# Zero-padding three small stationary operands to 128x128, and storing dt*x in three pieces, in a two-layer Mamba and outlook kernel

## The chip, the cores and the metric

The kernel runs on one core of a Trainium2 chip. The metric is the device time of one execution in microseconds (us); lower is better. Engines are named as the profile names them: PE (TensorE matmuls), PEld (its weight loads), DVE (VectorE), ACT (ScalarE), POOL (GpSimd) and SP, whose queue issues all DMAs of this kernel.

## The reference

The input x is (4, 384, 64, 64) in fp32. Two layers follow one another, each added to its input. The first is a selective state space layer (Mamba) over the 4096 pixels of an image taken as a sequence; the second is outlook attention, which the change does not touch. The first, cut to what matters:

```python
xz = einsum('blc,dc->bld', xn, in_proj_w)          # xn: normalised x; 2 x 768 channels
xb, z = split(xz, 2)
xc = silu(causal_conv4(xb) + conv_b)               # 768 channels
x_dbl = einsum('bld,ed->ble', xc, x_proj_w)        # 24 (dt) + 16 (B) + 16 (C)
dt = softplus(einsum('blr,dr->bld', x_dbl[..., :24], dt_w) + dt_b)
Bm, Cm = x_dbl[..., 24:40], x_dbl[..., 40:]
# for each time step, per channel d and state n (16 of them):
#   h = exp(dt * A) * h + (dt * xc) * Bm ;  y = sum_n h * Cm
y = (y + xc * D) * silu(z)
out = einsum('bld,cd->blc', y, out_proj_w)
```

## The kernel before, in words

**Tiling.** Each of the 4 images is cut into 17 chunks of 241 pixels (TM), 68 chunks in all. The 768 inner channels are NJ = 6 blocks of 128. A chunk is scanned in NU = 12 units of 64 channels; for one unit the scan state h is a tile of 128 partitions (4 states x 32 channels) by 8 segments of 242. The main loop runs over stages s, one unit per stage: DVE multiplies half of dt*x with B (`s_inputs2`), DVE scans (`s_scan`), POOL multiplies the other half with B (`s_inputs`) and the result with C (`s_outputs`), ACT makes the decay exp(dt*A) (`s_decay`), and at every odd stage PE sums h over the states for two units into a PSUM tile y (`s_sum`). The tiles h rotate through five buffers, so a multiply that begins a new h waits for the y matmuls that read the old one.

**Front work.** Everything that a chunk needs before its scan is put among the stages of earlier chunks by a dictionary written out by hand, `plan`. A key (r, part) gives a stage r, counted from two chunks before the chunk's own scan, and a place in it: EARLY, READY, SCAN, POOL, MID, LATE, in this order. As the chunk is 12 stages long, stages 18 and 6, for instance, fall together for two chunks. The entries that matter:

```python
(13, POOL): [at(f_silu, "xc", "zs")],
(14, POOL): [f_bc],
(15, EARLY): [f_xd],
(16, READY): [at(f_dt, 0)],
(16, SCAN): [at(f_dt, 1)],
(17, EARLY): [at(f_dt, 2)],
(17, READY): [at(f_plog, 0)],
(17, MID): [at(f_dtx, 0)],
(18, EARLY): [at(f_plog, 1)],
(18, SCAN): [at(f_dtx, 1), at(f_plog, 2)],
(19, READY): [at(f_dtx, 2)],
```

Every engine runs its instructions in the order of the program (`keep_in_program_order`).

**The steps.** `f_bc` multiplies xc with the x_proj weights wx into 56 rows of the PSUM tile px (ps_xd in the profile), six matmuls. `f_xd` has ACT copy these rows to the SBUF tile xd; rows 0 to 31 of it are B and C, 32 to 55 are dt, and the rest of its 64 rows stay at the 1.0 of a memset, so that row 56 carries the bias. `f_dt` (dt0, dt1, dt2 below) multiplies rows 32 to 56 of xd with wdt, two blocks at a time, into ps_dt; ACT takes the exponential. `f_plog` and `f_log` complete the softplus. `f_dtx` multiplies dt by xc on DVE, two blocks at a time, and after the third call the whole tile is stored to DRAM (dxd) with four DMAs of 32 partitions each, by `f_store`; `f_log` stores dt (dtd) in the same way. `f_b` spreads rows of B over 128 partitions by a matmul of xd with a 0/1 operand sel into bp. In the same stages lie `f_var` of a later chunk (ps_var, matmuls with one moving column), and `e_project` of an earlier one (ps_out). In fp32 the profile shows two matmul records for each matmul of the program.

**DMA order.** `s_fetch` brings dtx and dt of four 32-channel groups from DRAM to the layout of the scan (dxr, dtr), eight DMAs at every even stage, four units ahead of their scan, three buffers deep. All DMAs go through SP in program order. PSUM tiles of the front work (tag "mm") rotate through two buffers.

Of the kernel before, what the change touches and what calls it, by code (L numbers as in the profile page):

```python
# [7 lines left out]
F32 = mybir.dt.float32  # L8
# [4 lines left out]
P = 128  # L13
C = 384
NCB = C // P
DI = 768
NJ = DI // P
NS = 16
RK = 24
KC = 4  # L20
TM = 241
CG = 32
NQ = DI // CG
NG = NS // 4
# [55 lines left out]
def mamba_layer(ctx, tc, x, w, x1, sc1, bi1, consts, behind):  # L80
# [17 lines left out]
    pe, ve, ae, gp, sp = (  # L98
        InOrder(tc, e) for e in (nc.tensor, nc.vector, nc.scalar, nc.gpsimd, nc.sync)
    )  # L100
# [5 lines left out]
    wf = fronts.enter_context(tc.tile_pool(name="wf", bufs=1, side="right"))  # L106
    iof = fronts.enter_context(tc.tile_pool(name="iof", bufs=3, side="right"))
    front = fronts.enter_context(tc.tile_pool(name="front", bufs=1, side="right"))
# [3 lines left out]
    dram = ctx.enter_context(tc.tile_pool(name="dscr", bufs=3, space=bass.MemoryType.DRAM))  # L112
# [5 lines left out]
    def load(name, shape, pool=wp):  # L118
        t = pool.tile(shape, F32, tag=name, name=name)
        sp.dma_start(t, w[name])  # L120
        return t
# [62 lines left out]
    sp.dma_start(win[:, :, :DI], w["win"][:, :, :DI])  # L184
    cw = load("cw", [P, NJ, KC], wf)
    cbias = load("cbias", [P, NJ], wf)
    wx = load("wx", [P, NJ, 2 * NS + RK], wf)


    KX = 2 * NS + RK + 1  # L190
    xd = wf.tile([2 * CG, 1 + TM], F32, tag="xd", name="xd")
    gp.memset(xd, 1.0)
    wdt = wf.tile([KX, DI], F32, tag="wdt", name="wdt")
    sp.dma_start(wdt[2 * NS :, :], w["wdt"])
    alog = load("alog", [P, NQ, NG])
    sel = load("sel", [2 * NS, NG // 2, P], wf)

    cdiag = wf.tile([P, NJ, KC, P], F32, tag="cdiag", name="cdiag")
    ddiag = wp.tile([P, NJ, P], F32, tag="ddiag", name="ddiag")
# [190 lines left out]
    def f_bc(c):  # L390

        t = c.t
        px = pmm.tile([P, 2, TM], F32, tag="mm", name="ps_xd")
        for j in range(NJ):
            pe.matmul(
                px[: 2 * NS + RK, 0, :t], wx[:, j, :], c.xc[:, j, 1:], start=(j == 0), stop=(j == NJ - 1)
            )
        c.px = px

# [10 lines left out]
    def f_dt(c, jj):  # L410
        t = c.t
        if jj == 0:
            c.dt = front.tile([P, NJ, TM], F32, tag="dt", name="dt")
        pp = pmm.tile([P, 2, TM], F32, tag="mm", name="ps_dt")
        for h in range(2):
            j = 2 * jj + h
            pe.matmul(
                pp[:, h, :t], wdt[2 * NS :, j * P : (j + 1) * P], xd[2 * NS : KX, 1:], start=True, stop=True
            )
        ae.activation(c.dt[:, 2 * jj : 2 * jj + 2, :t], pp[:, :, :t], AF.Exp)  # L420

    def f_store(v, name):

        d = dram.tile([NJ, CG, 4, TM], F32, tag=name, name=name)
        for q in range(4):
            sp.dma_start(d[:, :, q, :].rearrange("j c t -> c j t"), v[CG * q : CG * (q + 1)])
        return d

    def f_log(c):

        t = c.t
        ae.activation(c.dt[:, :, :t], c.dt[:, :, :t], AF.Ln, bias=one)
        c.dtd = f_store(c.dt, "dtd")
# [15 lines left out]
    def f_b(c):  # L449

        for g in range(ND):
            pe.matmul(bp[:, g, : c.t], sel[:, g, :], xd[: 2 * NS, 1:], start=True, stop=True)

    def f_plog(c, jj):

# [2 lines left out]

    def f_dtx(c, jj):
        if jj == 0:  # L460
            c.dtx = front.tile([P, NJ, TM], F32, tag="dtx", name="dtx")
        ve.tensor_mul(c.dtx[:, 2 * jj : 2 * jj + 2, :], c.pl, c.xc[:, 2 * jj : 2 * jj + 2, 1:])
        if jj == NJ // 2 - 1:
            c.dxd = f_store(c.dtx, "dxd")

# [3 lines left out]
    def at(f, *args):  # L471
# [26 lines left out]
# [10 lines that stand above are left out]
        (19, POOL): [f_log],  # L508
        (19, MID): [f_spread],
# [52 lines left out]
    bp = pbb.tile([P, 2, TM], F32, tag="bp", name="bp")  # L562
# [188 lines left out]
    w_bias(NJ, 2 * NJ)  # L751
    w_scale(1)
    f_bc(first)
    f_xd(first)
    f_spread(first)
    for jj in range(NJ // 2):
        f_dt(first, jj)
    f_b(first)
    f_var(third)
    f_root(third)  # L760
# [15 lines left out]
    for s in range(-4, NU * (len(chunks) + 2)):  # L776
        k, m = divmod(s, NU)
# [53 lines left out]
class OutlookTile:  # L831
# [11 lines left out]
    def load(self, sp, x1, xr):  # L843

        c, W = self, self.W
        for cb in range(NCB):
            sp.dma_start(
                xr[:, cb, c.lo :, :],
                x1[c.b, :, (2 * NR * c.t + c.lo - 1) * W : (2 * NR * c.t + ROWS - 1) * W].rearrange(
                    "(p cb) (r w) -> p cb r w", cb=NCB, w=W  # L850
                )[:, cb],
            )
        self.xr = xr
# [357 lines left out]
def layers(ctx, tc, w, out):  # L1211
# [26 lines left out]

    started = []
    mamba_layer(tc, x.rearrange("b c h w -> b c (h w)"), w, x1, sc1, bi1, consts, behind)  # L1240
    outlook_layer(tc, x1, w, out, sc1, bi1, weights, ready)


def layouts(inputs):

    import numpy as np

    g = {k: np.asarray(v) for k, v in inputs.items()}
    c = np.ascontiguousarray

    def inner(v):
        v = v.reshape(NJ, P, *v.shape[1:])
        return c(np.swapaxes(v, 0, 1))

    a = {}
    a["x"] = c(g["x"])
    a["lnw"] = c(g["L0_conv_ln_w"].reshape(P, NCB))
    a["lnb"] = c(g["L0_conv_ln_b"].reshape(P, NCB))
    a["win"] = c(g["L0_conv_in_proj_w"].T.reshape(P, NCB, 2 * DI))
    a["cw"] = inner(g["L0_conv_conv_w"].reshape(DI, KC))  # L1260
    a["cbias"] = inner(g["L0_conv_conv_b"])
    wx = g["L0_conv_x_proj_w"]
    a["wx"] = inner(np.concatenate([wx[RK:], wx[:RK]], 0).T)
    a["wdt"] = c(np.concatenate([g["L0_conv_dt_w"].T, g["L0_conv_dt_b"][None]], 0))
    a["alog"] = c(
        g["L0_conv_A_log"].reshape(NQ, CG, NG, 4).transpose(3, 1, 0, 2).reshape(P, NQ, NG)
    )
    a["dvec"] = inner(g["L0_conv_D"])
    a["wout"] = c(inner(g["L0_conv_out_proj_w"].T).reshape(P, NJ, P, NCB).transpose(0, 1, 3, 2))

    wa = g["L1_conv_attn_w"].reshape(HEADS * KK, KK, C).swapaxes(0, 1).reshape(-1, C)
    a["wa"] = c(wa.T.reshape(P, NCB, -1))
    ab = g["L1_conv_attn_b"].reshape(HEADS * KK, KK).T.reshape(1, -1)
    a["ab"] = c(np.repeat(ab, P, 0))
    a["wv"] = c(g["L1_conv_conv_w"].reshape(KK, C, C).transpose(2, 0, 1).reshape(P, NCB, KK, C))
    wpr = g["L1_conv_proj_w"].T.reshape(NCB, P, P, NCB)
    a["wpr"] = c(wpr.transpose(1, 0, 3, 2))
    a["pb"] = c(g["L1_conv_proj_b"].reshape(P, NCB))
    f = np.float32
    a["ident"] = np.eye(P, dtype=f)  # L1280
    a["avg"] = np.full((P, P), 1.0 / C, f)
    a["blk12"] = np.kron(np.eye(P // 4, dtype=f), np.full((4, 4), 1.0 / 12.0, f)).astype(f)
    a["onesc"] = np.full((P, 1), 1.0 / C, f)
    r = np.arange(P)
    k = np.arange(2 * NS)
    a["sel"] = c(
        np.stack([(k[:, None] == 4 * i + r[None, :] // CG).astype(f) for i in range(NG // 2)], 1)
    )
    a["own"] = np.repeat(np.eye(GW, dtype=f), KK, 0)
    a["ssum"] = (r[:, None] % CG == np.arange(CG)[None, :]).astype(f)  # L1290
    return a
# [16 lines left out]
```

## Time and profile before

| | us |
|---|---|
| median of 3 runs | 6283.66 |
| the runs | 6276.35, 6283.66, 6298.06 |
| span of the profiled execution | 6278.2 |
| own time of the profiled execution | not listed beside its span |
| DVE h, the scan, busy | 3452.5 |
| POOL h, product with C, busy | 3225.4 |
| POOL h, product with B, busy | 1623.6 |
| PE ps_xd / ps_dt / bp, busy | 307.9 / 253.0 / 73.3 |
| first / last ps_xd | 84.1 / 4917 |

The profile is of one execution. "Busy" is the time in which an engine works on such instructions; idle time before a group is put down to whatever came last. The granted clock of PE is given per stretch, with 1.00 as full speed. In the timeline, each line has a start, a duration, the engine, the operation, the tiles as out<-in, the number of instructions merged, and in brackets the idle time ahead of it with its releaser. Sizes of matmul operands are written 25*128 for 25 rows by 128 columns of weights. Stretches and timelines below are in us from the start of the span.

### The profile page before, as it was taken

To read this page: it belongs to the slowest core of one execution; us is meant where nothing else is said; L and a number is where in the kernel's file an instruction comes from. 1 tells how busy PE (TensorE), PEld (TensorE's weight loads), DVE (VectorE), ACT (ScalarE), POOL (GpSimd) and SP (SyncE) were. 2 spreads that over 40 slices of the span, in tenths; PEclk is the share of its full clock that TensorE was granted. 3 is DMA by queue.
4 is the path that set the end of the run, shared out by engine and by line. 5 is a ranking of instruction groups with operands and counts; after the bars stand their busy time and mean duration, and the time that the engine had idled before them with its cause. 6 is when DMAs were issued, how large, how long until landed. Compare 5 with 4: busy or idle time off the path is not lost. (4 is left out here: it accounts for less than half of the span.)

```text
span 6278.2 us, 113454 instructions
## 1 busy us (share of the span) xinstructions
PE 5607.8 (89%) x40506; PEld 3965.2 (63%) x40506; DVE 5371.6 (86%) x4786; ACT 4990.9 (79%) x11842; POOL 5308.6 (85%) x2047
## 2 busy tenths in 40 slices
PE   6888988888888889988888888899888789999999
PEld 5666666666666666666666666666666455555555
DVE  4999999999999999999999999999999954445444
ACT  3888898888888888989888889888898845444544
POOL 3999999999999999999999999999999944433333
PEclk9999999899999999999999999999999899999999
DMA  4555555545555645555555545455545644454554
GB/s 128 133 134 147 146 135 133 133 129 143 147 138 132 146 129 138 146 132 136 141 137 147 140 126 136 129 134 139 135 125 135 167 149 162 165 170 165 173 169 146
DMA packets 640843, 894.22 MB, mean 142 GB/s; under 512 B 130249, under 2 KB 535163, under 8 KB 640148
## 3 DMA queue, kind: packets, MB, share of 16 engines
q1 hardware_dynamic: 640276, 886.96, 51.8%
q8 instruction: 319, 5.23, 0.4%
q14 instruction: 248, 2.03, 0.1%
HBM read 660.89 MB, written 225.70 MB: 141 GB/s over the span
## 5 line engine op out<-in xcount | busy, mean ns | idle before, releaser
L45 DVE TENSOR_TENSOR_SCAN h<-da,h 128x968 f32<-128x968 f32 x1632 | 3452.5, 2158 | 83.4 <-issue 48.5
L45 ACT ACTIVATE da<-dtr,aneg 128x241 f32<-128x241 f32 x6528 | 3036.8, 465 | 296.1 <-DVE h L45 133.5
L45 POOL TENSOR_TENSOR h<-h,bc 128x1928 f32<-128x1928 f32 x816 | 3225.4, 3953 | 12.7 <-DVE h L45 8.0
L45 POOL TENSOR_TENSOR h<-dxr,bc 128x964 f32<-128x964 f32 x816 | 1623.6, 1990 | 116.4 <-PE y L45 95.3
L45 PE MATMUL ps_in<-u,win 128*128 128x241 f32 x4896 | 1078.8, 374 | 83.4 <-DVE dtx L45 75.9
L45 PEld LDWEIGHTS ps_in<-u,win 128*128 128x128 f32 x4896 | 911.9, 191 | 248.2 <-DVE dtx L45 100.1
L45 POOL TENSOR_TENSOR bd<-ain,own 99x1188 f32<-99x1188 f32 x192 | 413.4, 2181 | 726.5 <-DMA ain<-ad 550.6
L45 DVE TENSOR_TENSOR h<-dxr,bp 128x964 f32<-128x964 f32 x816 | 931.6, 1142 | 109.2 <-PE y L45 93.8
L45 PE MATMUL y<-h,ssum 128*32 128x241 f32 x13056 | 907.2, 406 | 28.6 <-POOL h L45 27.7
L45 PEld LDWEIGHTS y<-h,ssum 128*32 128x32 f32 x13056 | 434.7, 119 | 442.8 <-issue 213.2
L45 PE MATMUL ps_cv<-xb,cdiag 128*128 128x241 f32 x3264 | 694.2, 368 | 5.7 <-ACT neg L45 4.7
L45 PEld LDWEIGHTS ps_cv<-xb,cdiag 128*128 128x128 f32 x3264 | 611.4, 189 | 78.5 <-issue 13.5
L45 PE MATMUL psv<-wv,xp 128*128 128x384 f32 x1728 | 592.8, 495 | 7.2 <-issue 7.2
L45 PE MATMUL ps_xd<-xc,wx 128*56 128x241 f32 x816 | 307.9, 559 | 323.1 <-ACT xc L45 323.1
L45 ACT ACTIVATE bd<-ain,own 99x324 f32<-99x324 f32 x704 | 334.6, 556 | 264.6 <-PE ps L45 240.6
L45 PE MATMUL ps_out<-zs,wout 128*128 128x241 f32 (+1 forms) x2448 | 537.2, 369 | 0.0
L45 DVE TENSOR_TENSOR fold<-fold,ps 128x192 f32<-128x192 f32 (+1 forms) x768 | 211.3, 303 | 333.2 <-PE ps L45 318.8
L45 PEld LDWEIGHTS ps_out<-zs,wout 128*128 128x128 f32 x2448 | 470.5, 192 | 36.5
L45 PEld LDWEIGHTS psv<-wv,xp 128*128 128x128 f32 x1728 | 322.7, 191 | 232.3 <-issue 18.1
L45 PEld LDWEIGHTS ps_xd<-xc,wx 128*56 128x56 f32 x816 | 154.6, 199 | 464.1 <-ACT xc L45 348.5
L45 ACT COPY vst<-psv 128x384 f32<-128x384 f32 x279 | 130.8, 470 | 322.3 <-PE psv L45 322.3
L45 PE MATMUL ps_dt<-xd,wdt 25*128 25x241 f32 x816 | 253.0, 436 | 113.5 <-ACT dt L45 80.4
(108 smaller groups left out, 5503.2 us busy)
## 6 DMA issues: line engine op xcount, KB each, us to landing
dxr<-dxd SPq DMA_DIRECT2D x1632, 120.5 KB
dtr<-dtd SPq DMA_DIRECT2D x1632, 120.5 KB
bc<-bcd SPq DMA_DIRECT2D x544, 120.5 KB
vin<-vd SPq DMA_DIRECT2D x384, 148.5 KB
vd<-vst SPq DMA_DIRECT2D x93, 576.0 KB
dxd<-dtx SPq DMA_DIRECT2D x272, 180.8 KB
dtd<-dt SPq DMA_DIRECT2D x272, 180.8 KB
xs<-in_x SPq DMA_DIRECT2D x96, 256.0 KB
```

Of the source, the lines that this page charges most:

```text
L45: return self.tc.keep_in_program_order(issue(*args, **kwargs))
```

## The change

The weights of x_proj (wx) get 72 zero columns, so that ps_xd has 128 rows; the weights of dt (wdt) get 32 zero rows ahead and 71 behind, and B's spread (sel) gets 96 zero rows behind, so that both multiply all 128 rows of xd, which grows to 128 partitions. ACT still copies 56 rows of ps_xd. The tile dtx becomes three tiles of two blocks in two buffers; each is stored with four DMAs as soon as it is written, where one store of the whole had followed the third.

```diff
-    wx = load("wx", [P, NJ, 2 * NS + RK], wf)
-    KX = 2 * NS + RK + 1
-    xd = wf.tile([2 * CG, 1 + TM], F32, tag="xd", name="xd")
+    wx = load("wx", [P, NJ, P], wf)
+    xd = wf.tile([P, 1 + TM], F32, tag="xd", name="xd")
     gp.memset(xd, 1.0)
-    wdt = wf.tile([KX, DI], F32, tag="wdt", name="wdt")
-    sp.dma_start(wdt[2 * NS :, :], w["wdt"])
+    wdt = load("wdt", [P, DI], wf)
     alog = load("alog", [P, NQ, NG])
-    sel = load("sel", [2 * NS, NG // 2, P], wf)
+    sel = load("sel", [P, NG // 2, P], wf)
...
-                px[: 2 * NS + RK, 0, :t], wx[:, j, :], c.xc[:, j, 1:], start=(j == 0), stop=(j == NJ - 1)
+                px[:, 0, :t], wx[:, j, :], c.xc[:, j, 1:], start=(j == 0), stop=(j == NJ - 1)
...
-                pp[:, h, :t], wdt[2 * NS :, j * P : (j + 1) * P], xd[2 * NS : KX, 1:], start=True, stop=True
+                pp[:, h, :t], wdt[:, j * P : (j + 1) * P], xd[:, 1:], start=True, stop=True
...
-    def f_store(v, name):
-
-        d = dram.tile([NJ, CG, 4, TM], F32, tag=name, name=name)
+    def store(v, d):
         for q in range(4):
             sp.dma_start(d[:, :, q, :].rearrange("j c t -> c j t"), v[CG * q : CG * (q + 1)])
+
+    def f_store(v, name):
+
+        d = dram.tile([NJ, CG, 4, TM], F32, tag=name, name=name)
+        store(v, d)
         return d
...
-            pe.matmul(bp[:, g, : c.t], sel[:, g, :], xd[: 2 * NS, 1:], start=True, stop=True)
+            pe.matmul(bp[:, g, : c.t], sel[:, g, :], xd[:, 1:], start=True, stop=True)
...
     def f_dtx(c, jj):
         if jj == 0:
-            c.dtx = front.tile([P, NJ, TM], F32, tag="dtx", name="dtx")
-        ve.tensor_mul(c.dtx[:, 2 * jj : 2 * jj + 2, :], c.pl, c.xc[:, 2 * jj : 2 * jj + 2, 1:])
-        if jj == NJ // 2 - 1:
-            c.dxd = f_store(c.dtx, "dxd")
+            c.dxd = dram.tile([NJ, CG, 4, TM], F32, tag="dxd", name="dxd")
+        dtx = front.tile([P, 2, TM], F32, tag="dtx", name="dtx", bufs=2)
+        ve.tensor_mul(dtx, c.pl, c.xc[:, 2 * jj : 2 * jj + 2, 1:])
+        store(dtx, c.dxd[2 * jj : 2 * jj + 2])
```

## The prediction

> **What bounds the kernel now.** I read the page first, then the busy time by stretch, the waits, and the timelines of two chunks.
>
> ```profile
> span 6278.2 us, 113454 instructions
> PE 5607.8 (89%) x40506; PEld 3965.2 (63%) x40506; DVE 5371.6 (86%) x4786; ACT 4990.9 (79%) x11842; POOL 5308.6 (85%) x2047
> ```
> ```profile
> 219.00:4841.00 4622.00, 4092.64 (x26733) 3029.72 (x26733) 4466.78 (x3362) 4121.19 (x9997) 4533.31 (x1617) 0.93 0.53 137
> ```
>
> The second fence is one stretch, the first layer in steady state; its columns are the length, then busy us of PE, PEld, DVE, ACT and POOL, the granted clock and DMA. POOL is busy 4533/4622 = 98%, DVE 97%, PE 89%. So the shares alone say that faster matmuls are worth nothing, and that at most the last 2% of POOL can be won. Who causes it is in the waits (total us, times, longest):
>
> ```profile
> POOL h L45 <- PE y L45: 95.3, 88, 8.1
> DVE h L45 <- PE y L45: 93.8, 111, 6.2
> ```
>
> The scan state h comes free only when the matmuls into y have read it, so a late y holds both full engines at once. By place in the chunk, 53.3 us of DVE's 93.8 are 39 waits at one spot, the y of stage 17, behind the last ps_dt; 30.2 us are waits of mostly 0.42 us two stages on, behind dtx and ps_in; the rest is the start. The distance from one chunk's ps_xd to the next is 71.4 us in chunks without the first wait and 71.4 plus that wait in the others (mean 72.2). So 53 us is what the changed matmuls can win there.
>
> Why is y late? A chunk with a wait of 1.24 us, PE first, then DVE and POOL:
>
> ```profile
> 937.64 4.48 PE L45 MATMUL ps_xd<-xc,wx 128*56 128x241 f32 x12 [4.75 <-ACT xc L45]
> ...
> 950.29 1.08 PE L45 MATMUL ps_dt<-xd,wdt 25*128 25x241 f32 x4 [1.19 <-ACT dt L45]
> 951.29 2.32 PE L45 MATMUL ps_var<-onesc,sq 128*121 128x1 f32 x12
> 953.55 1.97 PE L45 MATMUL ps_dt<-xd,wdt 25*128 25x241 f32 x4
> 955.44 1.17 PE L45 MATMUL y<-xc,ddiag 128*128 128x241 f32 x2
> 956.55 2.75 PE L45 MATMUL y<-h,ssum 128*32 128x241 f32 x32
> ```
> ```profile
> 959.34 1.16 DVE L45 TENSOR_TENSOR h<-dxr,bp 128x964 f32<-128x964 f32 x1 [1.24 <-PE y L45]
> 959.47 1.98 POOL L45 TENSOR_TENSOR h<-dxr,bc 128x964 f32<-128x964 f32 x1 [0.95 <-PE y L45]
> ```
>
> The same ps_dt group takes 1.08 us and then 1.97 us. The stretches (same columns) say why:
>
> ```profile
> 361.12:364.52 3.40, 3.02 (x8) 1.72 (x9) 3.40 (x5) 3.38 (x7) 3.40 (x1) 0.50 0.00 0
> 374.78:378.18 3.40, 3.03 (x20) 2.28 (x19) 3.40 (x3) 3.24 (x9) 3.40 (x2) 1.00 0.96 260
> 378.18:381.60 3.42, 3.42 (x29) 1.59 (x32) 3.42 (x2) 3.26 (x8) 3.42 (x2) 0.50 1.03 243
> 948.21:951.62 3.41, 2.22 (x12) 1.48 (x11) 3.41 (x2) 3.31 (x9) 3.41 (x2) 1.00 0.37 83
> 951.62:955.03 3.41, 3.41 (x15) 3.06 (x14) 3.41 (x3) 3.14 (x8) 3.41 (x3) 0.50 1.03 255
> ```
>
> The granted clock halves at 378.18 and at 951.62, in nearly every chunk just here. A first halving, while PE waits for the Silu, falls on ps_xd.
>
> [...] all changes of clock lie on one grid of 3.4133 us. [...] 361.12 (3.02 us of ps_xd, 128 rows, 56 columns) is followed by full clock, 374.78 (3.03 us of ps_dt, 25 rows, and ps_var, one moving column) by half. I count each 241-column matmul as 0.208 us (32 ps_cv in 6.67 us) times its share of rows in steps of 32, ps_var as nothing. Over 1437 windows a limit of 0.38 of the window then puts 15 on the wrong side, against 54 with all rows counted full. Columns must not be weighted: ps_xd brings the clock back. Zero weights seem to count: ps_cv, whose weights are diagonal, held 1.00 over two windows (2517.1 to 2523.9). [...]
>
> **The change part by part.**
> *ps_dt, 25 to 128 rows.* Four matmuls take 1.08 us now; at the full-array spacing (ps_in, 12 in 2.6 us, 0.22 each) about 0.1 us less. dt0 waits for ACT's copy, dt1 and dt2 mostly for ACT's exponential, so only dt2's 0.1 us reaches y: 7 us in 66 chunks. The real effect is activity. A window like 948.21, with four ps_out and four ps_dt, has (4 + 4/4) x 0.208 / 3.41 = 0.30 now and 8 x 0.208 / 3.41 = 0.49 then: it stays full, ps_var keeps 1.43 us instead of 2.3 to 2.4, dt2 about 1.0 instead of 1.97. The drop comes a window later and hits only y. That case exists today: the chunk at 361.50 has y alone at half clock, ends it 20.4 us after ps_xd's start, and DVE does not wait. What remains are phases whose window holds little but four ps_dt and ps_var (4 x 0.208 / 3.41 = 0.24), which start about 11.4 to 12.4 us after ps_xd: 1 of 3.41 us, 30%, half of it where dt2 lies outside the slow window; at 1.3 us (half-clock dt2 and most of y) 0.2 to 0.4 us per chunk. I take 0.32, also because 71.36 + 0.32 = 71.68 us is 21 windows, where the phase can lock. Saved: 53 - 66 x 0.32 = **32 us**, the 7 us included.
> *ps_xd, 56 to 128 columns.* Rows are unchanged, so activity is. Weight loads grow from 126 to about 190 ns, behind matmuls. [...] ACT copies ps_xd out only at 944.8, 2.7 us after its end. Cost nothing[...].
> *bp, 32 to 128 rows.* Four matmuls per chunk, 1.08 us to about 1.0, in a full stretch: nothing.
> *dtx in three pieces.* The same 60 KB x 12 in place of 180 KB x 4, so 8 DMA issues more per chunk. Four issues take 2.24 us on SP:
>
> ```profile
> 954.69 3.08 SPq L45 DMA_DIRECT2D dxr<-dxd  x4
> 957.88 2.09 SPq L45 DMA_DIRECT2D dtr<-dtd  x4
> 967.17 2.24 SPq L45 DMA_DIRECT2D dxd<-dtx  x4
> 975.90 2.21 SPq L45 DMA_DIRECT2D dtd<-dt  x4
> ```
>
> So +4.5 us, in SP's gaps (959.97 to 967.17 and 969.41 to 975.90). The first store moves ahead of the stage-18 fetch (954.69), which now waits behind DVE's first piece (957.44 to 958.09): stores to 960.3, fetch 960.3 to 965, about 5.5 us later. Its rows are needed by POOL two stages on, about 12 us after. Pieces two and three go out at 965.5 to 970, so dxd is complete 0.6 us later than now, but the next fetch waits for dtd, issued at 975.90, anyway. Nothing in steady state. New wait: two buffers for three pieces, so the third multiply waits for the first store. It starts 8.95 us (median, 7.7 least) after the first; 0.65 + 2.24 us of that go to multiply and issue, leaving 6.0 (4.8) us to land. A store of 361 KB (x1) lands in about 2.6 us. Hidden.
> *The start, once.* Loads grow by 0.22 + 0.32 + 0.10 = 0.64 MB ahead of x; at the 300 GB/s of 35 to 40 us that is 2.1 us, and PE waits for that x (1.03 us at 40.50). Twelve store issues end at 102.0 instead of 98.9 us, and the first dxr is waited for: 3 us. Together +5 us, between 0 and +8.
>
> Sum: -32 + 5 = **-27 us**. The profiled span is 6278.2 us; no execution time of its own is shown, and the runs have 6276.35 to 6298.06 with median 6283.66, so what lies around the span is small and I carry the difference over: **6257 us**. A measurement of this kernel tells about 0.3%, 19 us, from no change.
>
> **Rivals.**
> *Padding does not wake the clock* (rows that multiply zeros do not count, or rows 57 to 127, a constant one, do not). For it: no run here has padded rows; against it: ps_cv. Then only 0.1 us per chunk is won: -7 + 5, about 6282.
> *The wait moves into dtx, slower.* The third multiply is in DVE's order just ahead of the scans, and PE's ps_in, ps_rs and y wait for it, then POOL. Decided at a store landing time of 6.0 us; at 7 us, 1.0 us x 67 = +67, so -27 + 67 = +40: 6324. For it: the moved fetch puts 0.96 MB into the queues just behind that store, and DMA is at 1.03 of its share in this stretch. Against it: the store goes first, after the stage-16 fetch is through.
> *All of the late y goes:* -53 + 5 = 6236, if ps_var or loads also count.
>
> **How the numbers follow.** Main case 0.60 (6240 to 6268), no effect on the clock 0.22 (6274 to 6291), the wait in dtx or another new wait 0.15 (6300 to 6390), all gone 0.03. Four fifths of the main case pass 6264.8. Faster 0.50, same 0.33, slower 0.17. The range 6236 to 6294 leaves the slower cases out.
>
> **What would show it.** Right: in the changed profile the clock after ps_dt is full in more windows, "DVE h <- PE y" falls by about 30 us, ps_var stays near 1.43 us for 12, POOL's share of the steady stretch rises by half a per cent. Wrong: ps_dt at 1.97 us as often as now; DVE dtx waiting for a DMA; chunk distances that stay at 72.2 us, or a new floor above 71.4.

## The result, and the profile after

The changed kernel takes 6252.41 us (median of 6 runs, 6251.12 to 6258.35) against 6280.88 us of the kernel before in the same comparison (6 runs, 6267.06 to 6298.06): **ratio 0.9957 with an interval of 0.9943 to 0.9971**, 28.5 us less. The predicted difference was 27 us, and 0.43% lies above the 0.3% that a measurement can tell. The span of the profiled execution fell by 21.6 us; that execution is the slowest of the six (6258.35 us).

The page of the changed kernel gives the span, then the busy time of each engine:

```profile
span 6256.6 us, 114424 instructions
PE 5454.4 (87%) x40506; PEld 4053.0 (65%) x40506; DVE 5368.2 (86%) x4786; ACT 4987.6 (80%) x11842; POOL 5311.0 (85%) x2047
```

PE does as many matmuls as before in 153 us less busy time; DVE and POOL do the same work in the same time. The steady stretch of the first layer (length, then busy us of PE, PEld, DVE, ACT and POOL, granted clock, DMA):

```profile
219.00:4841.00 4622.00, 3961.99 (x26848) 3125.95 (x26849) 4487.05 (x3381) 4140.50 (x10050) 4559.65 (x1625) 0.95 0.52 137
```

The clock rose from 0.93 to 0.95 and POOL from 98.1% to 98.7% of the stretch. So the 153 us of PE were worth only what they freed on the two full engines, DVE and POOL; 1.3% of POOL is still open. The waits (total us, times, longest) show what was freed and what came new:

```profile
PE ps_out L45 <- DVE dtx L45: 93.7, 50, 2.9
...
POOL h L45 <- PE y L45: 75.4, 68, 8.1
...
DVE h L45 <- PE y L45: 59.2, 88, 6.2
...
DVE dtx L45 <- ACT ps_lg L45: 19.2, 22, 2.1
...
DVE dtx L45 <- DMA dxd<-dtx: 2.8, 1, 2.8
```

Two of these in the kernel before:

```profile
DVE dtx L45 <- ACT ps_lg L45: 6.0, 4, 2.1
PE ps_out L45 <- DVE dtx L45: 5.9, 4, 4.0
```

DVE's wait for y fell from 93.8 to 59.2 us. Of the 39 waits behind the last ps_dt (53.3 us), 15 are left (13.6 us). But DVE's wait for ps_lg, 6.0 us before, is 19.2 us now: 19 of these 22 waits lie in the steady chunks, 14.9 us against 1.9 (one wait) before.

**Where the new wait comes from.** Here is PE in a chunk whose clock stays full behind ps_dt (start, us, operation, in brackets the idle time ahead and its releaser):

```profile
2100.43 1.33 PE L45 MATMUL ps_var<-onesc,sq 128*121 128x1 f32 x12
2102.31 1.08 PE L45 MATMUL ps_dt<-xd,wdt 128*128 128x241 f32 x4 [0.55 <-ACT dt L45]
...
2103.73 1.84 PE L45 MATMUL y<-h,ssum 128*32 128x241 f32 x32
2107.47 1.07 PE L45 MATMUL ps_out<-xr,ident 128*128 128x241 f32 x2 [1.90 <-DVE dtx L45]
2108.34 3.94 PE L45 MATMUL ps_out<-zs,wout 128*128 128x241 f32 x12
```

The last ps_dt takes 1.08 us where the chunk shown of before had 1.97, ps_var takes 1.33 where it had 2.32, and y is done at 2105.6, 18.6 us after the start of ps_xd (2086.96). DVE does not wait for it. Now PE is too early: the next ps_out needs one of the two "mm" buffers, which DVE frees when its first dtx multiply has read it, so PE idles for 1.90 us (this wait has 93.7 us in all; before, it had 5.9). In this trace, as in that of before, every change of the granted clock lies within 0.002 us of a grid of 3.413 us; a window is one step of it. That idle time falls into one window, the second of these three (columns as above):

```profile
2100.79:2104.20 3.41, 2.86 (x28) 2.27 (x31) 3.41 (x3) 3.28 (x9) 3.41 (x3) 1.00 0.99 256
2104.20:2107.61 3.41, 1.51 (x29) 0.76 (x22) 3.41 (x5) 3.28 (x9) 3.41 (x1) 1.00 0.55 127
2107.61:2111.02 3.41, 3.41 (x9) 2.88 (x10) 3.41 (x4) 2.14 (x5) 3.41 (x4) 0.50 0.38 98
```

The first, with the last ps_dt on 128 rows in it and PE busy for 2.86 us, is followed by full clock. The second held 1.51 us of matmuls, and the third has half clock. It hits ps_out, 3.94 us for 12 instead of 2.61 one group later at 2113.23. ACT copies ps_out out and makes the last ps_lg after that, and DVE's third dtx waits for it; two lines of ACT's timeline and one of DVE's in the same chunk:

```profile
2112.31 0.36 ACT L45 COPY xr<-ps_out 128x241 f32<-128x241 f32 x1 [2.46 <-PE ps_out L45]
...
2114.66 0.66 ACT L45 ACTIVATE ps_lg<-dt,one 128x482 f32<-128x482 f32 x1
```
```profile
2115.35 0.66 DVE L45 TENSOR_TENSOR dtx<-ps_lg,xc 128x482 f32<-128x482 f32 x1 [0.79 <-ACT ps_lg L45]
```

The chunk is no exception. Of 65 chunks in this trace, 28 keep the clock from the last ps_dt to the end of the next ps_out. 18 lose it on the last ps_dt or on y, and all 15 waits for y lie in these. 19 lose it on ps_out alone, and 18 of the 19 new waits lie in these.

**The sum, from the traces.** The distance from one ps_xd to the next fell from 72.217 to 71.829 us. Over 65 distances that is 25.2 us, close to 39.7 us of waits saved less 13.0 new. The third ps_xd starts 2.1 us later (220.9 instead of 218.8 us), so the last one starts 23.1 us earlier, at 4889.75 instead of 4912.87 us (the 4917 in the table of before is the start of its last matmul). From there to the end it is 1366.9 us against 1365.3.

### The profile page after: what moved, and what is told of

It reads as the page before. It is cut to its first block, busy times and chain, and to the rows that moved or that the text cites. A ratio compares the mean times of both kernels' runs of the same rounds, so it can differ in the third digit from the quotient of the medians.

```text
span 6256.6 us, 114424 instructions
## 1 busy us (share of the span) xinstructions
PE 5454.4 (87%) x40506; PEld 4053.0 (65%) x40506; DVE 5368.2 (86%) x4786; ACT 4987.6 (80%) x11842; POOL 5311.0 (85%) x2047
## 5 line engine op out<-in xcount | busy, mean ns | idle before, releaser
L45 DVE TENSOR_TENSOR_SCAN h<-da,h 128x968 f32<-128x968 f32 x1632 | 3450.5, 2156 | 80.8 <-issue 48.1
L45 ACT ACTIVATE da<-dtr,aneg 128x241 f32<-128x241 f32 x6528 | 3036.7, 465 | 292.0 <-DVE h L45 130.1
L45 POOL TENSOR_TENSOR h<-h,bc 128x1928 f32<-128x1928 f32 x816 | 3229.6, 3958 | 10.7 <-DVE h L45 8.5
L45 POOL TENSOR_TENSOR h<-dxr,bc 128x964 f32<-128x964 f32 x816 | 1626.5, 1993 | 92.8 <-PE y L45 75.4
L45 PE MATMUL ps_in<-u,win 128*128 128x241 f32 x4896 | 1075.4, 373 | 78.5 <-DVE dtx L45 64.4
L45 PEld LDWEIGHTS ps_in<-u,win 128*128 128x128 f32 x4896 | 913.2, 190 | 235.8 <-DVE dtx L45 89.0
L45 POOL TENSOR_TENSOR bd<-ain,own 99x1188 f32<-99x1188 f32 x192 | 413.6, 2183 | 726.0 <-DMA ain<-ad 527.7
L45 DVE TENSOR_TENSOR h<-dxr,bp 128x964 f32<-128x964 f32 x816 | 928.8, 1138 | 74.6 <-PE y L45 59.2
L45 PE MATMUL y<-h,ssum 128*32 128x241 f32 x13056 | 847.6, 383 | 37.3 <-POOL h L45 37.3
L45 PE MATMUL ps_cv<-xb,cdiag 128*128 128x241 f32 x3264 | 694.1, 368 | 5.3 <-ACT neg L45 4.3
L45 PEld LDWEIGHTS y<-h,ssum 128*32 128x32 f32 x13056 | 416.0, 113 | 410.5 <-issue 153.2
L45 PEld LDWEIGHTS ps_cv<-xb,cdiag 128*128 128x128 f32 x3264 | 610.8, 189 | 78.4 <-issue 13.5
L45 PE MATMUL psv<-wv,xp 128*128 128x384 f32 x1728 | 591.4, 494 | 7.9 <-issue 7.9
L45 PE MATMUL ps_xd<-xc,wx 128*128 128x241 f32 x816 | 307.3, 556 | 323.1 <-ACT xc L45 323.1
L45 PE MATMUL ps_out<-zs,wout 128*128 128x241 f32 (+1 forms) x2448 | 561.6, 381 | 0.0
L45 ACT ACTIVATE bd<-ain,own 99x324 f32<-99x324 f32 x704 | 334.6, 556 | 262.6 <-PE ps L45 251.9
L45 PEld LDWEIGHTS ps_out<-zs,wout 128*128 128x128 f32 x2448 | 488.7, 200 | 43.1
L45 DVE TENSOR_TENSOR fold<-fold,ps 128x192 f32<-128x192 f32 (+1 forms) x768 | 211.3, 303 | 333.2 <-PE ps L45 318.8
L45 PEld LDWEIGHTS ps_xd<-xc,wx 128*128 128x128 f32 x816 | 239.5, 302 | 387.1 <-ACT xc L45 348.6
L45 PEld LDWEIGHTS psv<-wv,xp 128*128 128x128 f32 x1728 | 321.7, 191 | 232.5 <-issue 17.5
L45 ACT COPY vst<-psv 128x384 f32<-128x384 f32 x279 | 131.2, 471 | 323.0 <-PE psv L45 323.0
L45 PE MATMUL ps_dt<-xd,wdt 128*128 128x241 f32 x816 | 237.4, 418 | 153.0 <-ACT dt L45 108.3
```

The lines of the kernel that those rows point to most:

```text
L45: return self.tc.keep_in_program_order(issue(*args, **kwargs))
```

## The experiments

All ratios are against the kernel before in the same comparison, with intervals. The last four columns are worked out from the traces: the mean distance of successive ps_xd; DVE's waits for y behind the last ps_dt; DVE's dtx waiting for ps_lg in steady chunks; and the half-clock time between 8 and 29 us after ps_xd, per chunk, with the number of the 65 chunks that have none there. e7 and e8 have waits for y at a second place, the gate zs, which DVE computes from y; they stand apart. In e9 the first dummies carry the name of ps_xd and shift what is counted from it. Each trace is of one execution: for the changed kernel, e1, e6 and e11 it is the slowest of the runs, for e5 the fastest, and for e12 one of the fastest. So these columns tell where time goes, and the ratio tells how much.

| run | ratio | distance, us | y waits, us (times) | dtx waits, us (times) | half clock, us (chunks with none) |
|---|---|---|---|---|---|
| before | 1 | 72.217 | 53.3 (39) | 1.9 (1) | 5.83 (0) |
| after | 0.9957 [0.9943, 0.9971] | 71.829 | 13.6 (15) | 14.9 (19) | 2.77 (28) |
| e1_dt_rows | 0.9949 [0.9937, 0.9961] | 71.773 | 11.6 (14) | 12.6 (16) | 2.61 (28) |
| e2_after_dt_25rows | 1.0009 [0.9999, 1.0018] | 72.264 | 43.9 (34) | 1.4 (2) | 5.68 (0) |
| e3_pieces | 1.0007 [0.9999, 1.0015] | 72.189 | 45.3 (33) | 2.8 (2) | 5.53 (0) |
| e5_dt_64rows | 0.9967 [0.9955, 0.9980] | 71.849 | 28.2 (24) | 0.8 (1) | 4.57 (1) |
| e6_dt_zero_moving | 0.9939 [0.9924, 0.9955] | 71.788 | 14.0 (16) | 12.5 (16) | 2.55 (32) |
| e7_after_fill | 0.9943 [0.9929, 0.9958] | 71.754 | 1.8 (3); gate 18.5 (35) | 0 | 1.89 (30) |
| e8_before_fill | 1.0043 [1.0028, 1.0057] | 72.729 | 26.2 (20); gate 53.3 (64) | 0 | 4.36 (1) |
| e9_after_fill_silu | 0.9960 [0.9945, 0.9974] | 71.972 | not comparable | 0 | not comparable |
| e10_after_var_wide | 0.9941 [0.9927, 0.9954] | 71.693 | 0 | 23.6 (30) | 1.63 (34) |
| e11_dt_rows_var_wide | 0.9943 [0.9929, 0.9956] | 71.782 | 0 | 26.6 (34) | 1.89 (30) |
| e12_before_var_wide | 0.9992 [0.9984, 0.9999] | 72.030 | 40.0 (26) | 1.5 (2) | 3.32 (36) |
| **e13_dt_rows_var_wide_fill** | **0.9902 [0.9889, 0.9916]** | 71.317 | 0 | 1.6 (2) | 0.05 (64) |

### Which part of the change does it: e1, e2, e3

e1_dt_rows is the kernel before with ps_dt alone padded; x_proj, B's spread and dtx are as they were.

```diff
-    xd = wf.tile([2 * CG, 1 + TM], F32, tag="xd", name="xd")
-    wdt = wf.tile([KX, DI], F32, tag="wdt", name="wdt")
-    sp.dma_start(wdt[2 * NS :, :], w["wdt"])
+    xd = wf.tile([P, 1 + TM], F32, tag="xd", name="xd")
+    wdt = load("wdt", [P, DI], wf)   # 32 zero rows ahead, 71 behind
...
-    pp[:, h, :t], wdt[2 * NS :, j * P : (j + 1) * P], xd[2 * NS : KX, 1:], start=True, stop=True
+    pp[:, h, :t], wdt[:, j * P : (j + 1) * P], xd[:, 1:], start=True, stop=True
```

> Only ps_dt is padded, to 128 rows; x_proj, B's spread and the store of dtx are as before. Theory 1 (the clock counts the rows of a matmul, ps_dt was what let it fall): the whole gain of the change comes back, about -25 us or 0.9960, waits of DVE on y in stage 18 near 14 us (53 before), half clock in the stretch behind ps_dt near 2.8 us a chunk (5.8 before). Theory 2 ([...] each gains a little): a third of it, -8 us. Theory 3 (the earlier store of dtx gains): 0.

Theory 2 is that each of the three padded operands gains a little by itself.

e2_after_dt_25rows is the changed kernel with these lines turned back, so that all of the change but ps_dt is left.

> The changed kernel with ps_dt back at 25 rows; x_proj and B's spread stay padded and dtx stays in pieces. Theory 1: the gain is gone, 0 to +5 us against the kernel before, half clock near 5.8 us a chunk. Theory 2: two thirds of the gain stay, -17 us. Theory 3: all of it stays, -25 us.

e3_pieces is the kernel before with the three stores of dtx alone.

```diff
-            c.dtx = front.tile([P, NJ, TM], F32, tag="dtx", name="dtx")
-        ve.tensor_mul(c.dtx[:, 2 * jj : 2 * jj + 2, :], c.pl, c.xc[:, 2 * jj : 2 * jj + 2, 1:])
-        if jj == NJ // 2 - 1:
-            c.dxd = f_store(c.dtx, "dxd")
+            c.dxd = dram.tile([NJ, CG, 4, TM], F32, tag="dxd", name="dxd")
+        dtx = front.tile([P, 2, TM], F32, tag="dtx", name="dtx", bufs=2)
+        ve.tensor_mul(dtx, c.pl, c.xc[:, 2 * jj : 2 * jj + 2, 1:])
+        store(dtx, c.dxd[2 * jj : 2 * jj + 2])
```

> Only dtx in three pieces, no padding. Theories 1 and 2: no change within 0.2%, perhaps +2 to +3 us at the start (twelve store issues ahead of the first fetch in place of four). Theory 3: -25 us. If the third multiply waited for the first store, DVE dtx would show a wait on a DMA in every chunk and the time would rise by 67 us per us of it; theory 1 expects none.

Measured medians: 6246.97, 6284.28 and 6284.71 us, with the kernel before at 6279.25. The waits of e1, then one line each of e2's and e3's:

```profile
PE ps_out L45 <- DVE dtx L45: 90.8, 51, 3.7
...
DVE h L45 <- PE y L45: 54.8, 86, 6.2
...
DVE dtx L45 <- ACT ps_lg L45: 17.0, 19, 2.2
```
```profile
DVE h L45 <- PE y L45: 90.9, 107, 6.5
```
```profile
DVE dtx L45 <- DMA dxd<-dtx: 2.5, 1, 2.5
```

e1 has the whole gain, and with it the marks of the changed kernel: DVE's wait for y at 54.8 us, the new wait of ps_out for dtx, and behind it that of dtx for ps_lg. e2 has none of them: DVE waits 90.9 us for y, against 93.8 before, and ps_out 5.2 us for dtx. So the gain is ps_dt's rows alone; the columns of x_proj, the rows of B's spread and the pieces bring none that these runs can tell. In e3 DVE's dtx waits for a store once in the whole run, at the start. The pieces do save SBUF: by the sizes in the code, the two buffers of two blocks take 3.9 KB per partition where the whole tile took 5.8, while the wider wx takes 1.7 KB more. No run has all three operands padded and dtx in one tile. e1's median is 5.4 us below the changed kernel's, but the intervals of the ratios overlap.

### Rows, or the data in them: e5, e6

e5_dt_64rows reads 64 rows of xd with a 64-row wdt (32 zero rows ahead, 7 behind).

```diff
-    wdt[2 * NS :, j * P : (j + 1) * P], xd[2 * NS : KX, 1:]
+    wdt[:, j * P : (j + 1) * P], xd[: 2 * CG, 1:]
```

> Only ps_dt is padded, to 64 rows in place of 128 (32 zero rows ahead, 7 behind). Theory 1: each ps_dt counts half, so a window with four ps_out and four ps_dt has (4 + 2) x 0.208 / 3.41 = 0.37, just short of the limit of 0.38: the clock still falls in nearly every chunk, half clock 5 to 5.5 us a chunk, gain -5 to -10 us. [...]

e6_dt_zero_moving is e1 with `gp.memset(xd[2 * CG :, :], 0.0)`: rows 64 to 127 then multiply zero by zero, where e1 multiplied zero weights by the constant one.

> ps_dt padded to 128 rows alone, and rows 64 to 127 of the moving tile xd set to 0.0 in place of 1.0, so that half of the array multiplies zeros by zeros. Theory 1 with rows as such: as with ps_dt padded alone, about -25 us and half clock near 2.8 us a chunk. If what counts is data that toggles or is not zero: about 57 of 128 rows count, like 64 rows, -5 to -10 us and half clock above 5 us.

e6 measured 0.9939, the same as e1 within the intervals, with 14.0 us of y waits against 11.6. So padded rows did the same here with zeros in them as with ones: half clock of 2.55 us a chunk against 2.61. e5 measured 0.9967, more than was expected of it: all but one of its chunks still lose the clock, but for 4.57 us instead of 5.83, and that already halves the y waits (28.2 us). So the effect is graded in these runs: 5.83, 4.57 and 2.61 us of half clock a chunk with 25, 64 and 128 rows. It also has no dtx waits to speak of (0.8 us), but its net is smaller: by the medians it gains 19 us where e1 gains 32, though the intervals of the ratios overlap. Nor does e5 gain by shorter matmuls: at full clock, from the start of four ps_dt to the start of what follows, it takes 1.008 us in e5 and 1.006 before (medians); only 128 rows are shorter, 0.918 in e1.

### Filling PE's idle time with dummies: e7, e8, e9

e7_after_fill gives the changed kernel two dummy matmuls behind the first block of ps_out and four behind the y of stage 17, into halves of PSUM tiles that nobody reads. e8_before_fill has the same six in the kernel before.

```diff
+        ys = py.tile([P, 2, TM], F32, tag="y", name="y")
+        y = ys[:, 0]
...
+        if u.j == 1:
+            for _ in range(4):
+                pe.matmul(ys[:, 1, :t], ident, c.xc[:, u.j, :TM], start=True, stop=True)
...
+        if cb == 0:
+            for _ in range(2):
+                pe.matmul(po[:, 1, lo:], ident, c.xr[:, cb, lo:TM], start=True, stop=True)
```

> The changed kernel plus six matmuls per chunk whose results nobody reads: two behind the first ps_out (into the unused half of its PSUM tile, in PE's wait for ACT's exponential) and four behind the y of stage 17 (in the 1.9 us in which ps_out waits for dtx). Theory 1, with the later fall of the clock being what is left (DVE's new wait of 0.79 us for ps_lg): half clock behind ps_dt falls from 2.8 to under 1.5 us a chunk, both waits of DVE vanish nearly, the distance goes from 71.83 to about 71.4 us, -25 to -30 us against the changed kernel, 0.9915 against the kernel before. If more work on PE only costs: +6 x 0.42 x 67 = +170 us at worst where none of it lies in waits, or 0 where it does and the clock is not the cause.

> The kernel before, nothing padded, with the same six matmuls. Theory 1: the two ahead of the second ps_dt add 4 x 0.208 / 3.41 = 0.24 to one window, so the first fall of the clock comes later in many chunks, but the window with ps_var and 25-row ps_dt still trips it: waits on y fall from 0.82 to about 0.5 us a chunk, -15 to -25 us. Theory 2: no gain, or a loss of up to 170 us.

e9_after_fill_silu is e7 with nine more dummies ahead of ps_xd, while PE waits for the Silu.

```diff
+        for _ in range(9):
+            pe.matmul(px[:, 1, :t], ident, c.xb[:, 0, :t], start=True, stop=True)
```

> As the last but one, plus nine such matmuls ahead of ps_xd, in the 4.75 us in which PE waits for the Silu. Theory 1: ps_xd then runs at full clock in most chunks (2.6 in place of 4.4 us), but nothing waits for it except in chunks at the edge of a batch, so no more than -5 us against the kernel with six; if the slow ps_xd also sets what comes after, more.

One wait of DVE in the changed kernel, in e7 and in e8:

```profile
DVE zs L45 <- PE y L45: 8.7, 2, 8.1
```
```profile
DVE zs L45 <- PE y L45: 26.6, 39, 6.9
```
```profile
DVE zs L45 <- PE y L45: 61.3, 68, 6.9
```

e7's dtx waits are gone and its y waits nearly so, but its median of 6252.7 us is no better than the change without dummies. The gate zs takes back most of it: in 35 steady chunks it waits 18.5 us in all, and the trace names the last dummy as its releaser. It reads one half of the PSUM tile that the dummies write to in the other half; four of them, 1.89 us at full clock, end too late for it. e8 went the wrong way: 28 us slower than the kernel before, where a gain of 15 to 25 was expected. Its y still runs at half clock in 64 of 65 chunks and ends 20.8 us after the start of ps_xd in the mean, against 21.2 before and 19.5 in e7. The dummies come behind this late y, in 37 chunks partly at half clock too. Its y waits fall by 27.1 us, but its gate waits for 53.3. e9 has full clock during ps_xd, yet its runs (6257.04 to 6270.43 us) lie above those of e7 (6248.55 to 6254.28). An early ps_xd has nobody waiting; why it is slower is not settled.

### Moving columns of ps_var, and the best version: e10 to e13

The prediction counted ps_var, with its one moving column, as nothing. These kernels give it 112 columns of the same constant; one of them is read. The 0.093 us for 112 columns in the expectation of e10 is an estimate: 112/241 of the 0.20 us from one 241-column matmul to the next (0.203 in the median of ps_in at full clock, in the trace of before). A new line makes L45 of the views L46.

```diff
+VN = 112
-    onesc = load("onesc", [P, 1], wf)
+    onesc = load("onesc", [P, VN], wf)
-    pv[:n, i, 0:1], c.sq[:, cb, k0 : k0 + n], onesc, start=(cb == 0), stop=(cb == NCB - 1)
+    pv[:n, i, :VN], c.sq[:, cb, k0 : k0 + n], onesc, start=(cb == 0), stop=(cb == NCB - 1)
```

e10 is the changed kernel with it, e11 is e1 with it, e12 is the kernel before with it.

> The changed kernel with ps_var's moving operand 112 columns of ones wide in place of 1 (all columns of the result are equal, DVE reads the first). PE's 12 records stay bound by their weight loads (0.11 us each), but now stream 0.09 us each: 12 x 0.093 / 3.41 = 0.33 of a window. Theory 1: the clock no longer falls ahead of y, waits of DVE on y in stage 18 go from 13.6 to near 0; the fall moves to ps_out behind y (PE waits there for dtx) in up to half of the chunks, where it costs 0.79 us by ps_lg: 0 to -10 us against the changed kernel. If the clock did not follow what streams through the array: no change, or a loss where ps_var gets longer (up to 12 x 0.1 x 67 = 80 us).

> The kernel with ps_dt alone padded to 128 rows, with ps_var 112 columns wide; one store of dtx. Theory 1: as the changed kernel with ps_var widened, and about 5 us less for the shorter start: 6236 to 6248 us.

> The kernel before, no operand padded, with ps_var 112 columns wide. Theory 1: a window with ps_var and four 25-row ps_dt has 0.33 + 4/4 x 0.208 / 3.41 = 0.39, just at the limit of 0.38: the clock falls ahead of y in a quarter to a half of the chunks in place of nearly all, waits on y of 0.3 to 0.5 us a chunk in place of 0.82, -20 to -33 us: most of the gain of the change with nothing padded. If rows or tiling of ps_dt were the cause in itself: no gain.

e13 is e11 with two dummies behind the y of stage 17 (`range(2)` in the diff of e7, and none behind ps_out).

> As the last but one (ps_dt padded alone, ps_var wide), plus two matmuls that nobody reads behind the y of stage 17, into the unused half of its PSUM tile. Theory 1: with y always at full clock they end 0.9 us ahead of the gate that reads the tile, and keep the clock from falling on ps_out: the distance goes to about 71.3 us in nearly all chunks, 6225 to 6240 us. If the gate waits for them, 0.3 to 0.6 us a chunk are lost, +20 to +40 us.

e10's waits:

```profile
DVE h L46 <- PE y L46: 38.7, 71, 3.3
...
DVE dtx L46 <- ACT ps_lg L46: 28.5, 33, 2.7
```

No wait is left behind the last ps_dt in e10 and e11; what remains of 38.7 us are the two other spots. But the dtx waits grew to 23.6 and 26.6 us, and the medians, 6243.20 and 6244.45 us, do not separate from the changed kernel's and e1's. The loss had moved wholly to ps_out: in both traces, every chunk that loses the clock between the last ps_dt and the end of ps_out loses it on ps_out. e12 won next to nothing (0.9992), where a gain of 20 to 33 us was expected: 36 of its chunks keep the clock, but in the others it stays low for longer (7.4 us against 5.8 before), and 40.0 us of y waits remain. Its trace is of a better execution than most, with a clock of 0.947 where the median of its 21 runs is 0.943.

e13 closes the gap in front of ps_out, and the clock falls there in 1 of 65 chunks: **6219.49 us** (4 runs, 6218.33 to 6220.47) against 6277.90, the best kernel of the study and a little below the 6225 us that were expected at best. PE of one chunk, and the window that decides:

```profile
2090.20 1.84 PE L46 MATMUL y<-h,ssum 128*32 128x241 f32 x32
2091.97 1.08 PE L46 MATMUL y<-xc,ident 128*128 128x241 f32 x4
2093.93 0.67 PE L46 MATMUL ps_out<-xr,ident 128*128 128x241 f32 x2 [0.88 <-DVE dtx L46]
2094.44 2.61 PE L46 MATMUL ps_out<-zs,wout 128*128 128x241 f32 x12
```
```profile
2092.35:2095.76 3.41, 2.53 (x13) 2.03 (x12) 3.41 (x6) 3.25 (x9) 3.41 (x2) 1.00 1.05 246
```

ps_out still waits for dtx, but the dummies (the line with ident, four records for two matmuls) have filled the window, ps_out keeps 2.61 us, and the third dtx comes without a wait. The wait of dtx in e11, then in e13:

```profile
DVE dtx L46 <- ACT ps_lg L46: 31.5, 37, 2.7
```
```profile
DVE dtx L46 <- ACT ps_lg L46: 6.5, 5, 2.7
```

The two kernels differ by the two dummies alone: the wait is 25.0 us shorter, and so is the median time. The gate doesn't wait for two dummies (7.9 us in all, both waits in the last chunk). The distance is 71.317 us, at the floor of 71.4 us that the kernel before had in its chunks without a wait.

## Why the prediction was right, step by step

The mechanism was right up to y and wrong behind it. The sum came out at 27 us partly by luck, as two misses nearly cancel.

**ps_dt counts by its rows.** Shown by e1, e2, e5 and e6 (half clock of 2.61, 5.68, 4.57 and 2.55 us a chunk; 5.83 before). The first rival, that padding does not wake the clock, fell with e1 and e6. A ps_dt on 25 rows does not bring the clock down by itself: e12 leaves it so, and 36 of 65 chunks keep the clock. The prediction's count, which it calls activity, and its limit of 0.38 are the author's estimate, fitted to the trace of before alone, and not exact. A second count of that trace, with y's matmuls on 32 columns (32 in 1.84 us) taken as a quarter each, puts 25 of 1436 windows on the wrong side, against 69 with all rows counted full. The order is the same in e5 (19 against 49) and e12 (41 against 76).

**The 0.1 us of shorter matmuls.** Right: 0.918 us instead of 1.006 from the start of four ps_dt to the start of what follows, in the changed kernel as in e1.

**How much of the y wait goes.** This term was mis-sized: 21 us were to remain (0.32 us in 66 chunks) and 13.6 did, so 39.7 us went instead of 32. The share of bad chunks was right, 18 of 65 for the 30% that were forecast. The 0.32 was picked from a range of 0.2 to 0.4, in part because the chunk would then be 21 windows long; measured, it is 0.21.

**"The drop comes a window later and hits only y."** This step failed, and the miss went the other way. The chunk above shows the drop on ps_out, and DVE's third dtx waits behind it: 13.0 us of new waits, which the prediction had at none. The trace of before could have told that ps_out follows y on PE and that its buffers wait for dtx (5.9 us, above); the prediction stopped at y. That this wait was the next bound is shown by e11 and e13: with it gone, and the y waits too, the gain is about twice as large.

**ps_xd's columns, nothing.** Right: 307.3 us busy against 307.9. The weight loads grew, from 199 to 302 ns in the mean, without a longer row of matmuls. The matmuls after the change, then the loads after and before it (busy us, mean ns | idle before them and what ended it):

```profile
L45 PE MATMUL ps_xd<-xc,wx 128*128 128x241 f32 x816 | 307.3, 556 | 323.1 <-ACT xc L45 323.1
...
L45 PEld LDWEIGHTS ps_xd<-xc,wx 128*128 128x128 f32 x816 | 239.5, 302 | 387.1 <-ACT xc L45 348.6
```
```profile
L45 PEld LDWEIGHTS ps_xd<-xc,wx 128*56 128x56 f32 x816 | 154.6, 199 | 464.1 <-ACT xc L45 348.5
```

**bp's rows, nothing.** Right: its 272 matmuls went from 73.3 to 67.4 us busy, and e2, which keeps this edit, shows no gain.

**The pieces, nothing.** Right, by e3. SP of the changed kernel in one chunk:

```profile
957.11 1.75 SPq L45 DMA_DIRECT2D dxd<-dtx  x4
958.96 2.46 SPq L45 DMA_DIRECT2D dxr<-dxd  x4
...
963.56 4.03 SPq L45 DMA_DIRECT2D dxd<-dtx  x8
```

The order is the predicted one, the first store ahead of the fetch and two behind it. The issues cost 0.44 to 0.50 us each, a little less than the 0.56 that was taken from the whole stores. The rival in which the third dtx multiply waits for its store fell: 2.8 us, once, at 100.98 us. A wait in dtx did come, but for ps_lg.

**The start, +5 us.** Not settled. The third ps_xd comes 2.1 us later than in the trace of before, and PE waits for x 1.4 us longer. But over all the traces it lies between 216.0 and 221.6 us in no order of what was padded: e10, which has the whole change, has 216.2.

**All late y goes, 6236 us.** It did not: 15 waits stayed. In e10 all of them did go, and the time was 6243 us, with 23.6 us of waits for ps_lg in their place.

**A lock to 21 windows (71.68 us).** Not as a fixed length: of the 65 distances in the changed kernel, 8 lie within 0.1 us of 71.68, 25 are under 71.5 and 23 over 72. But ps_xd does gather at one place of the clock's window: 52 of its 66 starts fall into one third of it, against 28 in e13. Whether this is what sets the mean distances near 71.7 us of e1, e6, e7, e10 and e11 stays open, since no run isolates it.

Open are also why e9 is slower, and what the start costs.

## What to carry to other kernels

When PE is not the busiest engine but makes the busiest ones wait, look at its granted clock window by window, and pad small-row matmuls to the full array where the clock falls behind them: e1 (0.9949) cost a few zero rows and no PE time (ps_dt 236.9 us busy against 253.0). Then follow the freed time to the next thing in PE's order: a matmul group that comes earlier may only wait longer for its PSUM buffer (ps_out for dtx, 93.7 us instead of 5.9), and in 19 of 65 chunks the clock then fell on that group alone. A filler there must not delay the reader of its tile. Two dummies behind a y at full clock helped (e13, 25.0 us less than e11), four held up the reader (e7, 18.5 us of gate waits), and four behind a late y at half clock cost more than they gave (e8, 28 us slower than the kernel before).

## What the runs showed of the hardware

- In these runs the clock followed the rows that matmuls span, and not busy time alone. With PE busy for 3.03 of 3.40 us, ps_dt on 25 rows was followed by half clock in the kernel before (stretch 374.78); with PE busy for 2.86 of 3.41 us, ps_dt on 128 rows was followed by full clock in the changed kernel (stretch 2100.79). With 128 rows the y waits behind ps_dt went from 39 to 14 (e1), also where 64 of the rows held zeros on both sides (e6, 16).
- It followed the moving columns too: with 112 instead of 1 in ps_var and nothing else changed, 36 of 65 chunks of the traced execution kept the clock where none had (e12). They cost little at full clock, 1.42 us for 12 in e13's chunk against 1.33 to 1.43, and 123.8 us in total in e12, where part of them ran at half clock, against 118.4 before.
- A reader of one half of a PSUM tile waited for matmuls into its other half (e7: 26.6 us of waits in place of 8.7). Whether the chip or only this program asks for that wait, no run shows.
